# Decoder layer with experts: the last norm moved among the blocks of the last expert

## The chip, the core and the metric

The kernel runs on one core of a Trainium2 chip. The core has five engines with a queue of instructions each: TensorE (PE in the profile; PEld are its weight loads), VectorE (DVE), ScalarE (ACT), GpSimd (POOL) and SyncE (SP). In this kernel SP issues most plain transfers, and GpSimd issues the indirect ones, which gather or scatter rows by a table of row numbers. The metric is the time of one execution in microseconds; lower is better.

## The reference, cut to what matters

The reference is one decoder layer on 4 sequences of 512 tokens of 256 numbers: a state space mixer, an mLSTM attention over a context, and a feed-forward part with 8 experts, each followed by a residual addition and a layer norm. Only the last part matters here:

```python
logits = x @ gate_w
mult, sel = _sparse_mixer_routing(logits)       # two experts for each token
w = jnp.sum(mult[:, :, None] * (sel[:, :, None] == jnp.arange(E)[None, None, :]), axis=1)
h = jax.nn.silu(jnp.einsum('th,ehf->etf', x, w1)) * jnp.einsum('th,ehf->etf', x, w3)
out = jnp.einsum('etf,efh,te->th', h, w2, w)
...
x = _layernorm(x + _L0_ffn_ref(x, ...), axis=-1)
```

Each token goes through two of the eight experts; the two results, weighted, are added to the token's row, and the row is normed. There are 2048 rows, which the kernel handles as 16 tiles of 128.

## The kernel before, in words

After the first two layers, `close` writes the normed rows of each batch to `xd` (three copies in DRAM, of which the experts fetch) and to `yd`, the table in which the sums grow. `route` and `tables` put every token into lists: each expert has blocks of 128 tokens, with `tok` (which row to fetch), `wat` (which weight) and `dest` (which row to add to). Version 0 of the tables covers the first two batches, version 1 three, version 2 all four; version 3 holds overflow blocks, of which five (`NOV0`) are always run and up to 26 more behind a branch (L1668) that is not taken here.

A visit is an expert with one or more items; an item is one block of 128 rows or two. The order of visits is written by hand: `early` (experts 0 and 1, one block of version 0), `mid` (experts 2 to 7, blocks 0 and 1 of version 1), `late` (experts 6 down to 2, blocks 2 and 3, then the rest of experts 0 and 1, then the five overflow blocks). Each visit loads 3 MB of weights (`load_expert`, L1494, on SP, a ring of three). For each item, `fetch` gathers the rows (L1512, GpSimd), `turn` transposes them (L1578) and copies them out of PSUM (L1582), `up` multiplies by w1 and w3 (L1594), with Silu on ScalarE (L1599) and the product `ht` on VectorE (L1600), in four steps for a single block; three PSUM buffers (`pu`) stand between. `down` gathers the routing weights `wg` (L1611), multiplies by w2 (L1617), scales on ScalarE (L1621) and scatters with addition into `yd` (L1622). `work` runs `down` of an item after `up` of the next; the last `down` follows alone.

Only after all of this, and after the branch L1668, the sums are read back from `yd` into `x1` (L1676, four transfers of 512 KB), normed by `layer_norm` in four groups of four tiles (L63, L64, L66, L68, L73) and stored (L1681). A last branch (L1696) jumps over a slower exact form of the whole layer, which is not taken either.

The kernel is written with a framework that decides the order of the instructions on each engine by its own estimate of when each can start, and that adds the waits. What stands in the source in one place can therefore stand elsewhere on the engine's queue; where the text speaks of the built order, it means the order in the compiled program. [...] One case of this is the end of the second layer for batch 3: GpSimd adds the residual (L1076, four additions), VectorE takes its statistics (L63, `n2st`), while the first expert blocks already run on PE.

Of the kernel before, what the change touches and what calls it, by code (L numbers as in the profile page):

```python
# [9 lines left out]
F32 = mybir.dt.float32  # L10
AF = mybir.ActivationFunctionType
ALU = mybir.AluOpType
# [3 lines left out]
B, S, D = 4, 512, 256  # L16
# [26 lines left out]
def decoder_kernel(ctx: ExitStack, tc: tile.TileContext, t: dict, out: bass.AP):  # L43
    nc = tc.nc

    def pool(stack, name, bufs, psum=False):
        kw = {"space": PSUM} if psum else {}
        kw["reuse_waits"] = "tile"
        return stack.enter_context(tc.tile_pool(name=name, bufs=bufs, **kw))
# [28 lines left out]
    def layer_norm(sp, dst, src, n, tag):  # L78

        norm_apply(dst, src, n, *norm_stats(sp, src, n, tag))  # L80
# [1076 lines left out]
    def layers23(fast):  # L1157
# [4 lines left out]
        with ExitStack() as rest:  # L1162
# [360 lines left out]
            def static(v, e, *blocks):  # L1523
                return v, own(e, *blocks)

            early = [(e, [static(0, e, 0)]) for e in range(NEARLY)]
            mid = [(e, [static(1, e, 0, 1)]) for e in range(NEARLY, NE)]
            mid[-1][1].append(static(2, NE - 1, 2, 3))
            late = [(e, [static(2, e, 2, 3)]) for e in range(NE - 2, NEARLY - 1, -1)]
            late += [(e, [static(2, e, 1, 2), static(2, e, 3)]) for e in range(NEARLY)]  # L1530
            late += [((i,), [(3, [i])]) for i in range(NOV0)]
            rare = [((i,), [(3, [i])]) for i in range(NOV0, NOV)]

# [34 lines left out]
            xtp = pool(rest, "xt", 2)  # L1568
            np3 = pool(rest, "n3", 2)
            pup = pool(rest, "pu", 3, psum=True)  # L1570
# [13 lines left out]

            def up(xT_, G, w1, w3):

                N, U = G * P, TS // (G * P)
                ht = htp.tile([P, NF * G * P], F32, tag="ht", name="ht")
                for f in range(0, NF, U):
# [12 lines left out]
                    )  # L1602
                return ht.rearrange("p (f n) -> p f n", n=N)

            def down(v, cols, ht, w2):
                G = len(cols)
                ps = pop.tile([P, 2, D], F32, tag="po", name="po")
                y = yp.tile([P, 2, D], F32, tag="y", name="y")
                wg = xgp.tile([P, 2], F32, tag="wg", name="wg")
                for g, c in enumerate(cols):  # L1610
                    nc.gpsimd.indirect_dma_start(  # L1611
                        out=wg[:, g : g + 1], out_offset=None, in_=wds[min(v, 2)][:, :],
                        in_offset=bass.IndirectOffsetOnAxis(ap=wat[v][:, c : c + 1], axis=0),
                    )
                for g, c in enumerate(cols):
                    for f in range(NF):
                        nc.tensor.matmul(  # L1617
                            ps[:, g, :], ht[:, f, g * P : (g + 1) * P], w2[:, f, :],
                            start=(f == 0), stop=(f == NF - 1),
                        )  # L1620
                    nc.scalar.activation(y[:, g, :], ps[:, g, :], AF.Copy, scale=wg[:, g : g + 1])  # L1621
                    nc.gpsimd.indirect_dma_start(  # L1622
                        out=yd[:, :],
                        out_offset=bass.IndirectOffsetOnAxis(ap=dest[v][:, c : c + 1], axis=0),
                        in_=y[:, g, :], in_offset=None,
                        bounds_check=NT - 1, oob_is_err=False, compute_op=ALU.add,
                    )

            def work(visits, weights, ahead=(), between=None):


# [4 lines left out]
                for i, (n, v, cols) in enumerate(line):  # L1636
                    G = len(cols)
                    xT_ = turn(xgs.pop(0), G)
                    w1, w3, w2 = weights[n]
                    ht = up(xT_, G, w1, w3)  # L1640
                    if i + 2 < len(line):
# [6 lines left out]
                    if between is not None:  # L1648
                        between(i)
                down(*pending)  # L1650
                return weights[len(visits) :]

# [5 lines left out]
            else:  # L1658
                last = iter(())
            weights = work(early, weights, mid)  # L1660
            for _ in last:
                pass
            work(mid + late, weights, (), lambda i: overflow() if i == 1 else None)
            n_items = nc.values_load(
# [3 lines left out]
            with tc.If(n_items > NOV0):  # L1668
                work(rare, [weights_of(e) for e, _ in rare[:2]])


            NG = 4
            yv = yd.rearrange("(n p) d -> p n d", p=P)
            for g in range(NTT // NG):
                ns = slice(g * NG, (g + 1) * NG)
                nc.sync.dma_start(out=x1[:, ns, :], in_=yv[:, ns, :])  # L1676
            for g in range(NTT // NG):
                ns = slice(g * NG, (g + 1) * NG)
                ot = np3.tile([P, NG, D], F32, tag="ot", name="ot")
                layer_norm(np3, ot, x1[:, ns, :], NG, "n3")  # L1680
                nc.sync.dma_start(  # L1681
                    out=out_t[g * NG * P : (g + 1) * NG * P, :].rearrange("(i p) d -> p i d", p=P),
                    in_=ot,
                )

# [117 lines left out]
```

## Time and profile before

| What | us |
|---|---|
| Time, median of 3 runs (728.43 to 729.73) | 728.48 |
| The profiled execution's own time | 728.45 |
| Its span, first to last instruction | 726.5 |
| PE busy | 660.9 |
| VectorE busy | 303.9 |
| ScalarE busy | 230.7 |
| GpSimd busy | 220.7 |
| `up` matmuls (L1594), busy | 263.9 |
| `down` matmuls (L1617), busy | 135.3 |
| Scatters into `yd` (L1622), 37 of 1.61 | 59.7 |
| Mean granted clock of PE, as a share | 0.95 |

Busy times of engines overlap, so they do not add up to the span. What sets the end is read from two other views: the table of busy time in stretches of the execution, which tells where an engine has no gap, and the chain of work that ended last, which goes back from the last instruction to whatever released it. A line of the timeline shows start, duration, engine, line of the source, operation, what is written and read, and in brackets the idle time before it and what ended it. Lines with a q behind the engine are its sequencer: branches, semaphores, drains.

### The profile page before, as it was taken

The numbers are of one execution on the slowest core, as the hardware profiler recorded it, in microseconds if no ns is written. First come the engines' busy times: TensorE is split into PE (matmuls) and PEld (weight loads), VectorE is DVE, ScalarE is ACT, GpSimd is POOL, SyncE is SP. The second block draws the span as 40 slices with busy tenths as digits, with TensorE's granted clock in tenths as the row PEclk, the third lists the DMA queues.
The fourth block names the chain that finished last, engine by engine and source line by source line (L and its number), as shares of the span: only waits on it lengthen the run. The fifth ranks groups of instructions, "written<-read, shape, count | busy, mean of one in ns | idle before, by whom it ended". The sixth has DMA issues, their size and how long they took to land. (4 is left out here: it accounts for less than half of the span.)

```text
span 726.5 us, 8949 instructions
## 1 busy us (share of the span) xinstructions
PE 660.9 (91%) x3319; PEld 497.4 (68%) x3319; DVE 303.9 (42%) x776; ACT 230.7 (32%) x450; POOL 220.7 (30%) x244
## 2 busy tenths in 40 slices
PE   5979879998999898899999999999999999999930
PEld 2413357765534444888888888888888898999920
DVE  0796855668364787864222111112211211212116
ACT  1438760224357574552122111111212111212110
POOL 0512231000135466463232333322223232241210
PEclk9999988999989899899999999999999999999975
DMA  8200050100910325697445463454545634358234
GB/s 279 95 1 0 1 174 0 30 30 14 323 40 1 117 65 177 196 325 239 154 160 177 129 193 87 145 164 162 164 119 187 192 80 139 119 149 300 72 84 163
DMA packets 62895, 95.32 MB, mean 131 GB/s; under 512 B 8713, under 2 KB 49489, under 8 KB 62577
## 3 DMA queue, kind: packets, MB, share of 16 engines
q1 hardware_dynamic: 53456, 83.39, 33.7%
q0 software_dynamic: 8288, 9.08, 7.1%
q10 hardware_dynamic: 1088, 2.10, 0.9%
q8 instruction: 30, 0.49, 0.3%
q14 instruction: 33, 0.26, 0.1%
HBM read 81.40 MB, written 13.80 MB: 131 GB/s over the span
## 5 line engine op out<-in xcount | busy, mean ns | idle before, releaser
L1594 PE MATMUL pu<-xgT,w 128*128 128x256 f32 (+1 forms) x1472 | 263.9, 340 | 0.5 <-issue 0.4
L1594 PEld LDWEIGHTS pu<-xgT,w 128*128 128x128 f32 x1472 | 237.4, 192 | 24.8 <-issue 0.6
L1600 DVE TENSOR_TENSOR ht<-pu,si 128x256 f32<-128x256 f32 x148 | 62.7, 424 | 241.0 <-ACT si L1599 240.9
L1617 PE MATMUL po<-w,ht 128*128 128x256 f32 x592 | 135.3, 380 | 0.3 <-DVE ht L1600 0.3
L1622 POOL DMA_INDIRECT yd<-y,dest x37 | 59.7, 1613 | 206.5 <-ACT y L1621 183.6
L1599 ACT ACTIVATE si<-pu 128x256 f32<-128x256 f32 x148 | 56.7, 384 | 202.1 <-PE pu L1594 202.1
L1617 PEld LDWEIGHTS po<-w,ht 128*128 128x128 f32 x592 | 109.5, 190 | 15.5 <-DVE ht L1600 0.7
L202 PE MATMUL xz<-xT,win 128*128 128x512 f32 x128 | 60.1, 625 | 10.5 <-DMA win<-in_win 8.2
L202 PEld LDWEIGHTS xz<-xT,win 128*128 128x128 f32 x128 | 24.7, 198 | 44.3 <-issue 39.2
L1512 POOL DMA_INDIRECT xg<-xd,tok x37 | 36.8, 995 | 54.9 <-PE pt L1578 38.7
L1621 ACT ACTIVATE y<-po,wg 128x256 f32<-128x256 f32 x37 | 17.5, 474 | 106.3 <-PE po L1617 106.3
L981 POOL TENSOR_TENSOR ct<-ct,tri 128x128 f32<-128x128 f32 x64 | 32.7, 529 | 47.1 <-ACT ct L980 44.5
L1611 POOL DMA_INDIRECT wg<-wd,wat x37 | 37.3, 1009 | 11.1 <-issue 10.2
L418 PE MATMUL fpy<-mt,xs 128*128 128x512 f32 (+3 forms) x128 | 39.3, 460 | 0.9 <-DVE fsz L422 0.8
L221 DVE SCALAR_TENSOR_TENSOR acc<-xp,convw,acc 128x2048 f32<-128x2048 f32 x12 | 30.7, 2571 | 22.3 <-POOL acc L216 22.2
L980 ACT ACTIVATE ct<-pq,eT 128x512 f32<-128x512 f32 (+3 forms) x64 | 30.6, 523 | 22.8 <-PE pq L970 22.7
L970 PE MATMUL pq<-x1T,ctxT 64*128 64x512 f32 (+3 forms) x128 | 34.0, 505 | 3.3 <-ACT ct L980 3.2
L418 PEld LDWEIGHTS fpy<-mt,xs 128*128 128x128 f32 x128 | 23.2, 201 | 13.6 <-issue 7.3
L988 PE MATMUL ph<-ct,val 128*64 128x512 f32 (+3 forms) x128 | 32.4, 491 | 0.0
L1582 DVE COPY xgT<-pt 128x512 f32<-128x512 f32 (+1 forms) x23 | 13.5, 586 | 42.5 <-PE pt L1578 42.4
L439 PE MATMUL fpo<-fwout,fsz 128*128 128x256 f32 x128 | 29.7, 392 | 0.0
L970 PEld LDWEIGHTS pq<-x1T,ctxT 64*128 64x128 f32 x128 | 13.7, 193 | 22.8 <-ACT ct L980 10.9
(254 smaller groups left out, 596.9 us busy)
## 6 DMA issues: line engine op xcount, KB each, us to landing
w<-in_w SPq DMA_DIRECT2D x60, 1024.0 KB
xd<-x SPq DMA_DIRECT2D x9, 512.0 KB
xT<-in_xT ACTq DMA_DIRECT2D x4, 512.0 KB
ctxT<-in_ctxT SPq DMA_DIRECT2D x1, 2048.0 KB
val<-in_ctx SPq DMA_DIRECT2D x4, 512.0 KB
fxr<-in_x SPq DMA_DIRECT2D x4, 512.0 KB
yd<-x SPq DMA_DIRECT2D x4, 512.0 KB
x<-yd SPq DMA_DIRECT2D x4, 512.0 KB
```

Of the source, the lines that this page charges most:

```text
L202: nc.tensor.matmul(ps, win[:, k, c * P : (c + 1) * P], xT[:, k, b * S : (b + 1) * S], start=(k == 0), stop=(k == 1),)
L418: nc.tensor.matmul(ps[:, j * P :], xs[j][:, c, :], mt[b][j], start=(j == 0), stop=(j == NB - 1),)
L970: nc.tensor.matmul(ps[:, :w], ctxT[rows, p, s0 : s0 + P], x1T[rows, p, s0 : (b + 1) * S], start=True, stop=True,)
L981: nc.gpsimd.tensor_tensor(ct[:, :P], ct[:, :P], tri, ALU.mult)
L988: nc.tensor.matmul(po[DH * e : DH * (e + 1), tb * P :], val[:, b * NB + tb, 2 * p + e, :], cts[e], start=(tb == 0), stop=(tb == NB - 1),)
L1512: nc.gpsimd.indirect_dma_start(out=xg[:, g, :], out_offset=None, in_=xds[min(v, 2)][:, :], in_offset=bass.IndirectOffsetOnAxis(ap=tok[v][: ...
L1594: nc.tensor.matmul(ps[:, j, u, :], w[:, k, (f + u) * P : (f + u + 1) * P], xT_[:, k, :N], start=(k == 0), stop=(k == 1),)
L1599: nc.scalar.activation(si, ps[:, 0].rearrange("p u n -> p (u n)"), AF.Silu)
L1600: nc.vector.tensor_tensor(ht[:, f * N : (f + U) * N], ps[:, 1].rearrange("p u n -> p (u n)"), si, ALU.mult)
L1611: nc.gpsimd.indirect_dma_start(out=wg[:, g : g + 1], out_offset=None, in_=wds[min(v, 2)][:, :], in_offset=bass.IndirectOffsetOnAxis(ap=wat ...
L1617: nc.tensor.matmul(ps[:, g, :], ht[:, f, g * P : (g + 1) * P], w2[:, f, :], start=(f == 0), stop=(f == NF - 1),)
L1622: nc.gpsimd.indirect_dma_start(out=yd[:, :], out_offset=bass.IndirectOffsetOnAxis(ap=dest[v][:, c : c + 1], axis=0), in_=y[:, g, :], in_of ...
```

## The change

Expert 2 (`NEARLY`) leaves `mid` and `late` and becomes the visit `final`, with four items of one block each, behind the overflow blocks. `finale` runs it. The pending `down` of the last overflow block is issued inside the first of those blocks. Then the routing weights of all four blocks are gathered (`weigh`, into `wgf`), the sums of all 2048 rows are read back (`load_sums`), and the rows of the four blocks are gathered from `yd` into `ys`. From the second block on, each of the four steps of `up` is followed by a piece of `norm_all`: statistics of two tiles, then normed rows, half of them on VectorE (`apply`) and half on ScalarE (`apply2`), in place in `x1`, and the stores. So every row is normed and stored, also those to which expert 2 still has something to add. For these, `settle` adds the weighted product of the block to the gathered rows and takes their statistics, and `put` norms them and scatters them over the output. The branch for more overflow blocks comes last; if it were taken, the sums of expert 2 would be added to `yd`, and all rows would be normed and stored again.

In the listing of the diff, "..." marks what is left out; `normed` also holds the buffers, `down` now calls `weigh`, `product` and `scatter`, which do what its own lines did before.

```diff
-            mid = [(e, [static(1, e, 0, 1)]) for e in range(NEARLY, NE)]
+            mid = [(e, [static(1, e, 0, 1)]) for e in range(NEARLY + 1, NE)]
             mid[-1][1].append(static(2, NE - 1, 2, 3))
-            late = [(e, [static(2, e, 2, 3)]) for e in range(NE - 2, NEARLY - 1, -1)]
+            late = [(e, [static(2, e, 2, 3)]) for e in range(NE - 2, NEARLY, -1)]
             late += [(e, [static(2, e, 1, 2), static(2, e, 3)]) for e in range(NEARLY)]
             late += [((i,), [(3, [i])]) for i in range(NOV0)]
+
+            final = (NEARLY, [static(1, NEARLY, 0), static(1, NEARLY, 1)])
+            final[1].extend([static(2, NEARLY, 2), static(2, NEARLY, 3)])
             rare = [((i,), [(3, [i])]) for i in range(NOV0, NOV)]
...
-            np3 = pool(rest, "n3", 2)
+            np3 = pool(rest, "n3", 1)
+            fin = pool(rest, "fin", 1)
...
-            def up(xT_, G, w1, w3):
+            def up(xT_, G, w1, w3, ht):
 
                 N, U = G * P, TS // (G * P)
-                ht = htp.tile([P, NF * G * P], F32, tag="ht", name="ht")
...
-                return ht.rearrange("p (f n) -> p f n", n=N)
+                    yield
+
+            def inner(G):
+                return htp.tile([P, NF * G * P], F32, tag="ht", name="ht")
+
+            def weigh(wg, v, c):
+                nc.gpsimd.indirect_dma_start(
+                    out=wg, out_offset=None, in_=wds[min(v, 2)][:, :],
+                    in_offset=bass.IndirectOffsetOnAxis(ap=wat[v][:, c : c + 1], axis=0),
+                )
...
+            def product(ps, g, G, ht, w2):
+                for f in range(NF):
...
+            def scatter(rows, v, c, src, **kw):
+                return nc.gpsimd.indirect_dma_start(
+                    out=rows[:, :],
+                    out_offset=bass.IndirectOffsetOnAxis(ap=dest[v][:, c : c + 1], axis=0),
+                    in_=src, in_offset=None, bounds_check=NT - 1, oob_is_err=False, **kw,
+                )
...
-                down(*pending)
-                return weights[len(visits) :]
+                return weights[len(visits) :], pending
...
+                def stats(i, src):
+                    nc.vector.bn_stats(out=st[:, i, :], in_=src)
+                    nc.vector.bn_aggr(out=mv[:, i, :], in_=st[:, i, :])
+
+                def scales(i, j):
+                    nc.scalar.activation(sd[:, i:j], mv[:, i:j, 1], AF.Sqrt, bias=eps5)
+                    nc.vector.reciprocal(rs[:, i:j], sd[:, i:j])
+
+                def shifts(i, j):
+                    nc.vector.scalar_tensor_tensor(
+                        ms[:, i:j], mv[:, i:j, 0], -1.0, rs[:, i:j], ALU.mult, ALU.mult
+                    )
+
+                def apply(i, row, src=None):
+                    nc.vector.tensor_scalar(
+                        row, row if src is None else src, mv[:, i, 0:1], rs[:, i : i + 1], ALU.subtract, ALU.mult
+                    )
+
+                def apply2(i, row):
+                    nc.scalar.activation(
+                        row, row, AF.Identity, bias=ms[:, i : i + 1], scale=rs[:, i : i + 1]
+                    )
...
+            def load_sums():
+                for g in range(0, NTT, NG):
+                    nc.sync.dma_start(out=x1[:, g : g + NG, :], in_=yv[:, g : g + NG, :])
+
+            def store(g):
+                return nc.sync.dma_start(out=ov[:, g : g + NG, :], in_=x1[:, g : g + NG, :])
...
+            def finale(visit, weights, pending):
...
+                def norm_all():
+
+                    half = NTT // 2
+                    for h in range(2):
+                        for i in range(h * half, (h + 1) * half):
+                            stats(i, x1[:, i, :])
+                            if h and i % 2:
+                                apply(i - half - 1, x1[:, i - half - 1, :])
+                                apply2(i - half, x1[:, i - half, :])
+                                if i % NG == NG - 1:
+                                    store(i - half - NG + 1)
+                            if i % 2:
+                                yield
+                        if h == 0:
+                            scales(0, half)
+                            shifts(0, half)
+                    yield
+                    scales(half, NTT + 2)
+                    shifts(half, NTT + 2)
+                    for i in range(half, NTT, 2):
+                        apply(i, x1[:, i, :])
+                        apply2(i + 1, x1[:, i + 1, :])
+                        if i % NG == NG - 2:
+                            store(i + 2 - NG)
+                            yield
+                    for i in range(2):
+                        put(i)
+
+                def put(i):
+                    apply(NTT + i, ro[:, i, :], ys[:, i, :])
+                    v, (c,) = line[i]
+                    sent.append(scatter(out_t, v, c, ro[:, i, :]))
...
+                def settle(i, ps):
+                    nc.vector.scalar_tensor_tensor(
+                        ys[:, i, :], ps, wg[:, i : i + 1], ys[:, i, :], ALU.mult, ALU.add
+                    )
+                    stats(NTT + i, ys[:, i, :])
+
+                norm = norm_all()
+                xgs = [fetch(*it) for it in line[:2]]
+                hts = []
+                for i, (v, (c,)) in enumerate(line):
+                    xT_ = turn(xgs.pop(0), 1)
+                    hts.append(inner(1))
+                    for q, _ in enumerate(up(xT_, 1, w1, w3, hts[-1])):
+                        if q == 0:
+                            if i == 0:
+                                down(*pending)
+                                for j, (v_, (c_,)) in enumerate(line):
+                                    weigh(wg[:, j : j + 1], v_, c_)
+                                load_sums()
+                                for j, (v_, (c_,)) in enumerate(line):
+                                    nc.gpsimd.indirect_dma_start(
+                                        out=ys[:, j, :], out_offset=None, in_=yd[:, :],
+                                        in_offset=bass.IndirectOffsetOnAxis(
+                                            ap=tok[v_][:, c_ : c_ + 1], axis=0
+                                        ),
+                                    )
+                            else:
+                                ps = pop.tile([P, 2, D], F32, tag="po", name="po")
+                                product(ps[:, 0, :], 0, 1, hts[i - 1], w2)
+                                settle(i - 1, ps[:, 0, :])
+                            if i + 2 < N:
+                                xgs.append(fetch(*line[i + 2]))
+                        if i:
+                            next(norm, None)
+                for _ in norm:
+                    pass
+                scales(rows[N - 2], rows[N - 2] + 1)
+                put(N - 2)
+                ps = pop.tile([P, 2, D], F32, tag="po", name="po")
+                product(ps[:, 0, :], 0, 1, hts[-1], w2)
+                settle(N - 1, ps[:, 0, :])
+                scales(rows[N - 1], rows[N - 1] + 1)
+                put(N - 1)
+                return ys, sent
...
-            work(mid + late, weights, (), lambda i: overflow() if i == 1 else None)
+            weights, pending = work(
+                mid + late, weights, [final], lambda i: overflow() if i == 1 else None
+            )
+            ys, sent = finale(final, weights[0], pending)
             n_items = nc.values_load(
                 items, min_val=0, max_val=NOV,
                 skip_runtime_bounds_check_because="it is a sum of at most NOV items",
             )
             with tc.If(n_items > NOV0):
-                work(rare, [weights_of(e) for e, _ in rare[:2]])
-            NG = 4
-            yv = yd.rearrange("(n p) d -> p n d", p=P)
-            for g in range(NTT // NG):
-                ns = slice(g * NG, (g + 1) * NG)
-                nc.sync.dma_start(out=x1[:, ns, :], in_=yv[:, ns, :])
-            for g in range(NTT // NG):
-                ns = slice(g * NG, (g + 1) * NG)
-                ot = np3.tile([P, NG, D], F32, tag="ot", name="ot")
-                layer_norm(np3, ot, x1[:, ns, :], NG, "n3")
-                nc.sync.dma_start(
-                    out=out_t[g * NG * P : (g + 1) * NG * P, :].rearrange("(i p) d -> p i d", p=P),
-                    in_=ot,
-                )
+                for i, (v, (c,)) in enumerate(final[1]):
+                    scatter(yd, v, c, ys[:, i, :])
+                _, pending = work(rare, [weights_of(e) for e, _ in rare[:2]])
+                down(*pending)
+                stats, scales, shifts, apply, apply2 = normed(0)
...
```

## The prediction

> **What bounds the kernel now.** I read the table of busy time by stage first, then the chain that ended last, then the timeline of GpSimd, VectorE and PE around 310 to 320 us, then GpSimd's sequencer at the end. The stage table's columns are stretch, length, busy us of PE, PE's weight loads, VectorE, ScalarE, GpSimd, then PE's granted clock, DMA share and GB/s:
>
> ```profile
> 300.00:321.00 21.00, 20.73 (x160) 19.43 (x159) 13.56 (x66) 10.79 (x20) 12.20 (x13) 1.00 0.80 288
> 321.00:697.00 376.00, 374.76 (x1992) 334.24 (x1990) 81.17 (x211) 74.07 (x181) 117.93 (x98) 1.00 0.51 155
> 697.00:726.50 29.50, 0.00 (x0) 0.00 (x0) 12.39 (x52) 2.47 (x5) 1.56 (x1) 0.52 0.48 151
> ```
>
> The expert stage (321 to 697) is PE at full clock with hardly a gap: every us that PE is made to wait there is paid, and what other engines do beside it is free. Then come 29.5 us without PE. The chain (start, us, what) says what fills them:
>
> ```profile
> 682.67 20.21 DMA yd<-y,dest
> 702.88 0.02 issue
> 702.89 4.02 DMA x<-yd
> ...
> 719.41 0.41 DVE ot L73
> ```
>
> PE's last product ends at 696.15 (its group starts at 689.94 and lasts 6.21); the last scatter starts at 697.43 and lands 3.7 later; the sums are read back from 702.89; VectorE norms from 706.93 to 719.82; then 6.7 us for the last store and the program's end. That tail is 726.5 - 696.15 = 30.35 us.
>
> GpSimd's own end is off the path today, but it decides what follows:
>
> ```profile
> L1668 POOLq INC_SWDGE_SEM  x1: 1574/1574/1574, 701.4 to 701.4; - x1
> L1696 POOLq COMPARE_BRANCH  x1: 45/45/45, 703.4 to 703.4; - x1
> L1696 POOLq EVENT_SEMAPHORE  x6: 17/30/43, 707.7 to 708.2; - x6
> L1799 POOLq DRAIN  x1: 5750/5750/5750, 709.8 to 709.8; - x1
> ```
>
> (ns min/median/max, first and last start.) After its last scatter lands (701.2) its queue passes the unused branch L1668 (1.57 us of semaphore work), jumps over the exact path (L1696, 703.4 to 707.7), does 1.57 us more and drains until 715.55: 14.3 us from landing to drained. The final barrier takes 0.8 us after the last arrival (725.7 to 726.5).
>
> **The change, part by part.** Blocks of expert 2 are 0 to 3; t counts from block 0's first up-projection matmul.
>
> *Expert 2 goes last, in four single blocks.* A double visit takes PE 21.16 us (381.10 to 402.26, from one up-projection to the next, is the row), a single block 10.82 (671.98 to 682.80): 4 x 10.82 - 2 x 21.16 = +0.95 us. One load of 3 MB falls away; PE waits for no weights now, so that is worth nothing. Where t = 0 lies: the last overflow item's up-projection moves from 682.80 to 640.48; 7.14 us of it, 2.6 of the product before, 0.22 of transposes and 0.87 of its own product put t = 0 at 651.3, other delays not counted.
>
> *Weights of expert 2's rows gathered early.* In the built order the two gathers of wgf for blocks 0 and 1 stand on GpSimd's queue directly ahead of the residual additions of batch 3 (L1076), behind two like them of today:
>
> ```profile
> 311.95 0.94 POOL L1611 DMA_INDIRECT wg<-wd,wat  x1 [0.30 <-issue]
> 312.92 2.79 POOL L1076 TENSOR_TENSOR hv<-hv,x 128x256 f32<-128x256 f32 x4
> 313.69 0.43 DVE L63 BATCH_NORM_STATS2 n2st<-hv 128x6 f32<-128x256 f32 x1 [2.95 <-POOL hv L1076]
> 318.93 0.42 DVE L1600 TENSOR_TENSOR ht<-pu,si 128x256 f32<-128x256 f32 x1
> 319.41 1.13 PE L1617 MATMUL po<-w,ht 128*128 128x256 f32 x4 [0.28 <-DVE ht L1600]
> ```
>
> hv starts the moment GpSimd is free; VectorE waits for it, and behind that wait stands the product ht for which PE already waits. Two gathers at 0.94 + 0.31 us are +2.5 us on PE's path; 0 if something else were late too, 2.8 at most. No gap after 322 gives it back. The wgf gathers of blocks 2 and 3 wait for the last routing tables (written by 333.4), where GpSimd then idles until 356: nothing.
>
> *The norm of all rows inside the last blocks.* The last overflow product ends at t = 4.38; its scatter starts at 5.2 and lands at 8.95. The read-back is issued then, at 9.1, no longer behind the L1668 branch; its first quarter is there 4.02 later (t = 13.2), the others 1.5 us apart (0.5 MB at the 345 to 376 GB/s of 705 to 710). GpSimd's four row gathers wait for the same landing; behind them stand only the output scatters, since the blocks' rows are fetched ahead; gathers of this size land 4.3 after issue, so the first is there at 13.5. In the built order VectorE takes six statistics ahead of ht of block 1's first quarter, and all of the following ahead of the copy of block 2's transposed rows: sixteen statistics at 0.39, three ht at 0.40, the first settle 0.45 with its statistic 0.39, four applies at 0.33, two small ones 0.33, the copy 0.42: 10.35 us, so the copy ends at 23.6 to 24.2. PE wants it at 2 x (1.79 + 2.59 + 5.36) + 2 x (0.22 + 0.86) = 21.64. PE stands 2.2 us; 1.5 if the quarters come early, 4 if the row gathers push in front of them. The other waits are covered: three PSUM buffers let ht of block 1 come at 18.8 (it comes at 15.9); ScalarE's seven more table loads (1.28 us each, the row at 306.39) and eight Identity rows of 0.53 end before the ht that needs them; the stores are issued by t = 36 and land by 41, and three of the four output scatters (1.9 us each) follow by 47.
>
> *The tail.* PE ends at 4 x 9.74 + 3 x 1.08 + 3.45 + 2.2 = 47.85. Settle 0.45, statistics 0.39 + 0.17, root 0.30, reciprocal 0.18, apply 0.41, semaphores and issue 0.55: the last scatter starts 2.5 later. It lands in 3.7 (the row of the last yd scatter; 3.2 to 5.2 over the quiet ones), and now GpSimd's end is on the path, 14.3 + 0.8. The tail is 2.5 + 3.7 + 15.1 = 21.3 us against 30.35: -9.05.
>
> Here the Trainium skill is weighed ("VectorE: DVE Perf Modes", The DRAIN you can't avoid): it gives the drains of the program's end as some 12 ns, constant, on all five engines. Four engines agree (7 to 17 ns), GpSimd's row is 5750. By the rule the tail would be 15.6 us; I take the row, since the same instructions stand ahead of it in both kernels.
>
> Sum: -9.05 + 0.95 + 2.5 + 2.2 = -3.4. Span 726.5 - 3.4 = 723.1; the profiled execution took 728.45 for its 726.5, with the median of the runs at 728.48, so 723.1 + 1.95 = 725.1 us.
>
> **PE's clock.** Both stalls cut dense matmuls for 2 to 3 us. The skill ("TensorE: Matmul & The Clock Gate", Why this matters for your kernels) allows gaps up to about 3 us before a window of idling halves the clock; by it they cost only themselves. The trace shows less patience:
>
> ```profile
> 241.00:242.00 1.00, 0.03 (x1) 0.06 (x1) 1.00 (x2) 1.00 (x4) 0.95 (x1) 0.53 0.00 0
> 247.00:248.00 1.00, 1.00 (x4) 0.78 (x5) 1.00 (x5) 0.34 (x2) 0.00 (x0) 0.56 1.05 344
> ```
>
> The granted clock (third from the end) fell to half with a gap of 1.2 us behind it and one of 1.9 just begun, and came back 6.8 us later; around 288, with PE as idle, it stayed whole. A fall costs PE half of 3.4 to 6.8 us, 1.7 to 3.4. By the rule the sum stays at -3.4, by the row it is up to +3.4; I keep the rule for the likeliest number and put the row into the range.
>
> **Rivals.** (1) *Slower than before, through the clock*: both stalls halve it for 6.8 us each: 725.1 + 2 x 3.4 = 731.9. It decides once it costs 4.9 us, one long fall and one short. For it the fall at 241; against, no single gap in dense work has an example here. (2) *A longer stall ahead of block 2*: the read-back's quarters wait behind the row gathers; 3 us more gives 728.1, no change. For it: beside weight loads a scatter took 7.8 us to land; against: no weights are loading then. (3) *GpSimd's drain belongs to something that no longer runs*: 725.1 - 5.7 = 719.4. (4) *The early gathers are hidden*, a part that does nothing: 722.6.
>
> **How the numbers follow.** My forecast, with rival 4 and up to one short fall of the clock, 722 to 727: 0.54. Rival 3: 0.12, all faster. Rival 2, between 727 and 730: 0.13. Rival 1 and still longer stalls, above 730: 0.21. A measurement of this kernel can't tell 0.2% (1.5 us) from nothing, so faster is below 727.0 and slower above 730.0: 0.66, 0.13, 0.21. The range, 719.4 to 731.0, leaves out half of rival 1 and part of rival 3.
>
> **What would show it.** Right: VectorE's first n2st of batch 3 at about 316.2 after 5.4 us of waiting for hv; PE idle near 319 to 322; one gap of some 2 us ahead of block 2, ended by the copy of transposed rows; the last output scatter near 704; a chain that ends in GpSimd's queue with a drain of 5 to 6 us. Wrong: PE gap-free in the last expert, a clock below 1.00 after a gap, stores landing after the last scatter could start, or a drain of some ns.

## The result and the profile after

The changed kernel takes 719.15 us (median of 4 runs, 718.58 to 719.62); the kernel before took 728.45 beside it (727.90 to 729.73). The ratio is 0.987, with a 95% interval of 0.9852 to 0.9887. Forecast were 725.1 us and a range of 719.4 to 731.0: the direction was right, the gain of 9.3 us is nearly three times the 3.4 us that I had summed, and the time lies just below the range. The profiled execution took 718.58 for a span of 716.7 (forecast 723.1).

The table of busy time by stage of the changed kernel, with the columns as for the kernel before (length; busy us of PE, its weight loads, VectorE, ScalarE, GpSimd; PE's granted clock, DMA share, GB/s):

```profile
300.00:321.00 21.00, 18.49 (x137) 17.05 (x136) 12.93 (x63) 9.38 (x17) 13.13 (x14) 1.00 0.80 282
321.00:701.20 380.20, 378.65 (x2131) 340.75 (x2131) 95.33 (x271) 87.25 (x198) 118.26 (x100) 1.00 0.51 157
701.20:716.70 15.50, 0.00 (x0) 0.00 (x0) 1.67 (x5) 0.29 (x1) 0.98 (x1) 0.60 0.08 17
```

PE stays the bound to 701.2, some 5 us longer than before, and the stretch without PE shrank from 29.5 us to 15.5, of which VectorE works 1.67. The chain that ended last (start, us, what) now ends in GpSimd's work:

```profile
658.94 3.69 DMA yd<-y,dest
...
663.61 6.66 DMA x<-yd
...
676.47 0.34 DVE xgT L1586
676.82 0.14 issue
676.95 2.02 PE pu L1597 x16
...
697.74 3.47 PE po L1619 x16
701.21 0.02 issue
701.24 0.50 DVE ys L1763
...
703.42 0.50 POOLq L1822
703.92 0.71 POOL out L1625
```

The scatter of the last overflow block lands at 662.63, a load of the sums lands at 670.27, VectorE's statistics and rows follow, and the copy of block 2's transposed rows ends at 676.81; PE has waited 1.54 us for it. The timeline shows this wait, and the earlier one of VectorE for the residual rows (`hv`), behind the early gathers:

```profile
315.10 0.43 DVE L63 BATCH_NORM_STATS2 n2st<-hv 128x6 f32<-128x256 f32 x1 [5.46 <-POOL hv L1076]
...
676.95 2.02 PE L1597 MATMUL pu<-xgT,w 128*128 128x128 f32 x16 [1.54 <-DVE xgT L1586]
```

Behind PE's last product come settle, statistics, root, apply and the last scatter. Its issue starts at 703.65 on the timeline; the chain puts the start 0.27 later. What follows on GpSimd's sequencer (ns min/median/max, first and last start; the drain line also holds two short ones) is not in the chain, but takes the rest of the span:

```profile
L1826 POOLq EVENT_SEMAPHORE  x4: 17/43/4112, 704.5 to 708.8; - x4
L1826 POOLq INC_SWDGE_SEM  x1: 598/598/598, 708.9 to 708.9; - x1
L1859 POOLq COMPARE_BRANCH  x1: 45/45/45, 709.9 to 709.9; - x1
L1859 POOLq EVENT_SEMAPHORE  x6: 17/30/43, 713.0 to 713.4; - x6
L1859 POOLq INC_SWDGE_SEM  x1: 576/576/576, 713.5 to 713.5; - x1
L1962 POOLq DRAIN  x3: 46/107/1748, 714.1 to 716.4; - x3
```

The same instructions as before, with other lengths: the two semaphore steps take 0.60 and 0.58 us instead of 1.57 each, the drain 1.75 instead of 5.75. From the landing (708.8) to the end of the drain (715.85) it is 7.1 us, where I had put 14.3.

### The profile page after: what moved, and what is told of

Its sections match the earlier page's. It is cut to its first block, busy times and chain, and to the rows that moved or that the text cites. A ratio compares the mean times of both kernels' runs of the same rounds, so it can differ in the third digit from the quotient of the medians.

```text
span 716.7 us, 9223 instructions
## 1 busy us (share of the span) xinstructions
PE 663.3 (93%) x3447; PEld 502.6 (70%) x3447; DVE 307.1 (43%) x788; ACT 240.2 (34%) x460; POOL 220.4 (31%) x248
## 5 line engine op out<-in xcount | busy, mean ns | idle before, releaser
L1597 PE MATMUL pu<-xgT,w 128*128 128x128 f32 (+1 forms) x1600 | 266.6, 327 | 1.6 <-DVE xgT L1586 1.5
L1597 PEld LDWEIGHTS pu<-xgT,w 128*128 128x128 f32 x1600 | 243.2, 193 | 23.9 <-ACT si L1602 1.9
L1625 POOL DMA_INDIRECT yd<-y,dest x33 | 53.3, 1616 | 146.6 <-ACT y L1639 127.0
L1639 ACT ACTIVATE y<-po,wg 128x256 f32<-128x256 f32 x33 | 15.6, 474 | 92.5 <-PE po L1619 92.5
L1612 POOL DMA_INDIRECT wg<-wd,wat x33 | 32.6, 989 | 9.9 <-issue 9.6
L1586 DVE COPY xgT<-pt 128x256 f32<-128x256 f32 (+1 forms) x25 | 13.8, 551 | 41.6 <-PE pt L1582 41.6
```

The costliest lines, as they stand in the source:

```text
L1597: nc.tensor.matmul(ps[:, j, u, :], w[:, k, (f + u) * P : (f + u + 1) * P], xT_[:, k, :N], start=(k == 0), stop=(k == 1),)
L1612: nc.gpsimd.indirect_dma_start(out=wg, out_offset=None, in_=wds[min(v, 2)][:, :], in_offset=bass.IndirectOffsetOnAxis(ap=wat[v][:, c : c + ...
L1625: return nc.gpsimd.indirect_dma_start(out=rows[:, :], out_offset=bass.IndirectOffsetOnAxis(ap=dest[v][:, c : c + 1], axis=0), in_=src, in_ ...
```

## The experiments

The experiments ran on different chips, on which the kernel before took from 727.8 to 735.3 us. Times are therefore compared only with runs beside them on the same chip, and most readings are lengths inside a trace. The listings of the edits are shortened.

### What sets the length of GpSimd's end: four suspects taken one at a time

The kind of the last transfer, in the changed kernel and, turned round, in the kernel before:

```diff
-                    sent.append(scatter(out_t, v, c, ro[:, i, :]))
+                    kw = dict(compute_op=ALU.add) if i == N - 1 else {}
+                    sent.append(scatter(out_t, v, c, ro[:, i, :], **kw))
```

> The changed kernel, with one difference: the last of the four output scatters adds to the rows it meets, as the scatters into yd do (so the rows of that block come out as a sum of two normed rows). Theory A (the kind of GpSimd's last transfer sets how long its end takes): the issue takes 1.6 us, the two semaphore steps 1.57 each, the drain 5.75; from landing to drained 14.3 us instead of 7.1, span 716.7 + 0.6 + 7.2 = 724.5. Theory B (VectorE's work beside it slows GpSimd's end) and theory C (the transfers of the sums and of the output beside it do): steps of 0.6, drain of 1.75, span 717.3.

```diff
+                    kw = dict(compute_op=ALU.add) if adds else {}
...
-                        bounds_check=NT - 1, oob_is_err=False, compute_op=ALU.add,
+                        bounds_check=NT - 1, oob_is_err=False, **kw,
...
-                down(*pending)
+                down(*pending, adds=between is None)
```

> The kernel before, with one difference: the last scatter of the last overflow block writes its rows instead of adding them (so those rows lack their other parts). Theory A: the two semaphore steps fall to 0.6 us each and the drain to 1.75, though the norm still follows; GpSimd is done at about 708 instead of 715.6, and the time is at most 1 to 1.5 us shorter (an issue of 1.0 instead of 1.6, and the read-back stands behind the first semaphore step), since VectorE sets the end. Theories B and C: steps of 1.57, drain of 5.75, GpSimd done at 715.

VectorE's work and the transfers beside it:

```diff
-                ot = np3.tile([P, NG, D], F32, tag="ot", name="ot")
-                layer_norm(np3, ot, x1[:, ns, :], NG, "n3")
...
-                    in_=ot,
+                    in_=x1[:, ns, :],
```

> The kernel before without the last norm: the sums are read back and stored as they are, so VectorE has nothing to do after 697 us. Theory B: GpSimd's drain falls to about 1.75 us. Theory A: it stays at 5.75, the semaphore steps at 1.57, and GpSimd's 715.6 + 0.8 sets the end near 716.4 to 718. Theory C: the drain stays long where the stores run beside it, and ends with them, near 715.

```diff
                 put(N - 1)
+                idle = fin.tile([P, 40, 6], F32, tag="idle", name="idle")
+                for i in range(40):
+                    nc.vector.bn_stats(out=idle[:, i, :], in_=ys[:, N - 1, :])
```

> The changed kernel, with 40 statistics of one and the same tile on VectorE behind the last output row (their results are not used): VectorE is busy from 703.4 to about 719 us, all through GpSimd's end. Theory B: semaphore steps of 1.57 and a drain above 5 us, GpSimd's end at 723, span 724. Theories A and C: steps of 0.6, drain of 1.75; VectorE's own end sets the span near 720 to 722.

Measured, in that order (kernel before beside them: 730.08): 719.35, 728.11, 722.61 and 722.62 us. The sequencer's drain in each, `last_adds`:

```profile
L1963 POOLq DRAIN  x3: 46/107/1748, 714.9 to 717.2; - x3
```

`last_plain`:

```profile
L1800 POOLq DRAIN  x3: 46/107/5750, 709.4 to 725.9; - x3
```

`no_last_norm`:

```profile
L1797 POOLq DRAIN  x3: 46/107/5750, 710.6 to 720.3; - x3
```

`vector_busy`:

```profile
L1965 POOLq DRAIN  x3: 46/107/1748, 717.5 to 720.5; - x3
```

To the nanosecond, each has the drain of the kernel that it was made from, and the first semaphore step too; the second differs by 2 to 4 ns (the two steps take 598 and 580, 1574 and 1565, 1574 and 1565, 598 and 580). A last transfer that adds or one that writes, VectorE busy or idle, many transfers beside it or fewer: none moves it. Theories A and B fall with this. In `vector_busy` VectorE ran to 719.25 while the drain began at 717.5. Against theory C stands that in `no_last_norm` the DMA share was 1.09 from 710 to 715, during the drain, against 0.46 in the kernel before, and the drain kept its length; `before_4_more`, below, settles it. What was left is something that the two programs differ in as a whole. The profile's list of transfers gives one: the kernel before issues 111 indirect transfers (37 each of `xg`, `wg`, `yd`), the changed one 115 (37, 33 and 33, and 4 each of `wgf`, `ys`, `out`).

### The number of indirect transfers

Further gathers of 128 weights, not used, each with one of the visits 6 to 11 of the list (counted from 0), where GpSimd idles:

```diff
                     if between is not None:
                         between(i)
+                        for k in range(n):      # n = 1, 4; in the changed kernel 13
+                            if i == 6 + k % 6:
+                                spare = xgp.tile([P, 2], F32, tag="spare", name="spare")
+                                nc.gpsimd.indirect_dma_start(
+                                    out=spare[:, 0:1], out_offset=None, in_=wds[2][:, :],
+                                    in_offset=bass.IndirectOffsetOnAxis(ap=wat[2][:, 0:1], axis=0),
+                                )
```

> The kernel before with one more indirect gather of 128 weights (not used), in the middle of the expert stage where GpSimd idles: 112 indirect transfers instead of 111. The first runs had semaphore steps of 1.57 us and a drain of 5.75 in every form of the kernel before, and of 0.6 and 1.75 in every form of the changed kernel, which issues 115. Theory D (the number of indirect transfers issued so far sets it): other values than 1.57 and 5.75, on a line through 111 and 115: 1.33 and 4.75. Theory E (it belongs to the code around the branches, not to the number): 1.57 and 5.75. The time is 728.5 to 730 in both.

> The kernel before with four more such gathers: 115 indirect transfers, as many as the changed kernel has. Theory D: semaphore steps of 0.6 us and a drain of 1.75, GpSimd done near 708.5. Theory E: 1.57 and 5.75, GpSimd done near 715.6. The time stays at 728.5 to 730, since VectorE sets the end here.

> The changed kernel with 13 more such gathers: 128 indirect transfers. Theory D: semaphore steps and drain change; where to depends on where the count starts again, with the end of the span moved by as much (a drain of 5.75 and steps of 1.57 would give 716.7 + 6 = 722.7). Theory E: 0.6 and 1.75, span 716.7 to 717.5.

They took 727.06, 726.45 and 719.81 us (kernel before beside them 728.23). `before_1_more` missed the straight line of theory D (steps of 1594 and 1585, drain 5832: up, not down), but it moved; `before_4_more` has the changed kernel's short end in the old program, with the last norm, the read-back and the stores all beside it as before:

```profile
L1675 POOLq INC_SWDGE_SEM  x1: 584/584/584, 700.2 to 700.2; - x1
L1806 POOLq DRAIN  x3: 46/107/1707, 706.4 to 724.4; - x3
```

and `after_13_more` is longer again, 818 and 2647. So the length goes up with further transfers, and down once between 112 and 115. Theories C and E are out. Two more runs, n = 2 and 3 in the kernel before, place the fall:

> The kernel before with two more gathers of 128 weights: 113 indirect transfers. The semaphore steps took 1574, 1594 and 584 ns at 111, 112 and 115 transfers, the drain 5750, 5832 and 1707. Theory D as a sawtooth that falls once between 112 and 115: either 1614 and 5914 (one more step of 20 and 82 up the line), or, if the fall is already past, 540 and 1540. An estimate puts the fall between: the Trainium skill (DMA Engines, The descriptor swizzle) counts 9 descriptors on each of the 16 engines for a transfer over 128 partitions, so that 113 transfers make 1017 and 114 make 1026; if the queue holds a round 1024, 113 is still long.

> The kernel before with three more such gathers: 114 indirect transfers. By the same estimate (1026 descriptors, past 1024): the fall is past, semaphore steps near 564 ns, drain near 1625. If the fall lies between 114 and 115: 1634 and 5996.

`before_2_more` (113 transfers):

```profile
L1675 POOLq INC_SWDGE_SEM  x1: 1614/1614/1614, 704.3 to 704.3; - x1
L1806 POOLq DRAIN  x3: 46/107/5913, 712.8 to 728.8; - x3
```

`before_3_more` (114 transfers):

```profile
L1675 POOLq INC_SWDGE_SEM  x1: 574/574/574, 707.4 to 707.4; - x1
L1806 POOLq DRAIN  x3: 46/107/1667, 714.4 to 731.4; - x3
```

| Indirect transfers | First step, ns | Drain, ns | Kernel |
|---|---|---|---|
| 111 | 1574 | 5750 | before, and two variants of it |
| 111 | 1588 | 5791 | `plain_weights` (below) |
| 112 | 1594 | 5832 | before, 1 more |
| 113 | 1614 | 5913 | before, 2 more |
| 114 | 574 | 1667 | before, 3 more |
| 115 | 584 | 1707 | before, 4 more |
| 115 | 598 | 1748 | changed, and its variants with 115 |
| 128 | 818 | 2647 | changed, 13 more |

One step over the edge takes 1.04 us from each semaphore step and 4.25 from the drain, 6.3 together. At an equal number the changed program is still 14 ns longer in the first step and 41 in the drain than the kernel before (both at 111 and at 115), so the number is nearly, but not quite, all that counts. The added transfers, and those taken away, were all gathers of 128 weights; transfers of another shape were not tried.

The edge lies where the estimate in the expectation had it. The Trainium skill ("DMA: Bandwidth & Descriptors", The descriptor swizzle) counts 9 read and 9 write descriptors per engine for one transfer of 1 MiB to 128 partitions. Taken over, as an estimate, for each of these smaller transfers, that makes 1017 for 113 of them and 1026 for 114. That they fill a ring of 1024 entries fits, but it stays a guess: only one edge was seen, and no trace here counts descriptors. These two runs took 731.17 and 733.94 us (kernel before 731.15); in the kernel before, GpSimd's end is covered, so their times say nothing of it.

### Back to 111 in the changed kernel, and the two other terms

The four gathers of `wgf` as plain loads of SyncE; the same four from the last tables; each block transposed during the block before; and the last two together:

```diff
-                                    weigh(wg[:, j : j + 1], v_, c_)
+                                    nc.sync.dma_start(out=wg[:, j : j + 1], in_=wds[min(v_, 2)][0:P, :])
```

> The changed kernel, with the four gathers of wgf replaced by plain loads on SyncE's queue (the first 128 entries of the weight table instead of the listed ones, so expert 2's part is weighted wrongly). 111 indirect transfers, as in the kernel before. Theory D (GpSimd's end grows with the number of indirect transfers and falls somewhere between 112 and 115): semaphore steps of 1.57 us and a drain of 5.75 are back, 5.9 us more at the end than the changed kernel has. The two gathers ahead of the residual additions are gone too: PE comes out of that place 1.4 us earlier by the trace of the changed kernel, 2.5 by my prediction. Sum 719.2 + 5.9 - 1.4 = 723.7, or 722.6. Theory E (the drain belongs to the code around the branches): 719.2 - 1.4 = 717.8, or 716.7.

```diff
-                                    weigh(wg[:, j : j + 1], v_, c_)
+                                    weigh(wg[:, j : j + 1], 2, c_)
```

> The changed kernel, with all four gathers of wgf made from the last routing tables, so that none can stand ahead of the residual additions of batch 3; still 115 indirect transfers. My prediction's term: 719.2 - 2.5 = 716.7. By the changed kernel's trace (PE stands 2.13 + 0.38 us there, 0.28 before, and its next up-projection is 1.85 later relative to the kernel before, of which the front's own drift is open): 719.2 - 1.4 to - 2.2 = 717.0 to 717.8. The rival that these gathers are hidden: 719.2.

```diff
+                ahead = turn(xgs.pop(0), 1)
                 for i, (v, (c,)) in enumerate(line):
-                    xT_ = turn(xgs.pop(0), 1)
+                    xT_, ahead = ahead, None
                     hts.append(inner(1))
                     for q, _ in enumerate(up(xT_, 1, w1, w3, hts[-1])):
+                        if q == 0 and i + 1 < N:
+                            ahead = turn(xgs.pop(0), 1)
```

> The changed kernel, with each block's rows transposed and copied while the block before begins, so that the copy of block 2's rows no longer stands behind sixteen statistics on VectorE. My prediction's term (2.2) as the trace of the changed kernel has it: PE's gap of 1.54 us ahead of block 2 goes, 719.2 - 1.5 = 717.7. Rival: the wait returns at another place, since the product ht stands behind the same statistics and ScalarE's Silu behind their root: 719.2.

> The changed kernel with both edits: wgf gathered from the last tables, and each block's rows transposed while the block before begins. The two places do not touch each other, so the gains add: 719.2 - 1.4 - 1.5 = 716.3, or 715.2 with my prediction's 2.5 for the gathers. If one of them is given back at the end: 717.7.

Medians: 724.56 (718.09 to 727.59), 719.76 (718.45 to 720.65), 723.07 (719.25 to 725.12) and 719.31 (716.03 to 722.22), with the kernel before at 733.01 (731.40 to 735.13). Spreads this wide, and no run of the changed kernel beside them, decide little by time. `plain_weights` decides by its trace: with 111 transfers the changed program has the long end back.

```profile
L1826 POOLq INC_SWDGE_SEM  x1: 1588/1588/1588, 710.1 to 710.1; - x1
L1859 POOLq INC_SWDGE_SEM  x1: 1566/1566/1566, 715.2 to 715.2; - x1
L1962 POOLq DRAIN  x3: 46/107/5791, 716.8 to 723.1; - x3
```

From the start of its last scatter (705.49) to the end of the span (723.4) it takes 17.9 us; `late_weights`, with 115, takes 12.2 (705.80 to 718.0). The two steps make 2.0 of the difference of 5.7 and the drain 4.0; the jump over the exact path is 0.4 shorter.

For the other two terms the runs were repeated on one chip, with the changed kernel beside them:

> The changed kernel itself, so that the next three can be held against it on one chip: 719.2, if this chip is like the first.

> The changed kernel with all four gathers of wgf made from the last routing tables. Counted within one trace, the way from the product group ahead of the place (309.35 before, 308.26 after) to the first up-projection of the next visits (321.98, 323.83) took 12.63 us before and 15.57 after, and two groups further 19.21 and 22.61; PE's granted clock fell to 0.74 and 0.83 there. If the two gathers are the cause of both, the way takes 12.6 and 19.2 again, the clock stays at 1.00, and the time is 3.4 us below the changed kernel's. My prediction's term: 2.5 below it. If they are hidden: the same.

> The changed kernel with each block's rows transposed while the block before begins. On the earlier chip PE's gap ahead of the up-projection of block 2 did not go: it was 1.17 to 1.21 us and ended by the product ht instead of the copy. So the rival (the wait returns at another place): 0.3 us below the changed kernel; my prediction's term as measured: 1.5 below it.

> Both edits together: 3.4 + 0.3 = 3.7 us below the changed kernel if the gathers cost 3.4 and the stall only moves, 4.9 if the stall goes. A ratio of 0.982 to 0.981 to the kernel before.

Changed kernel 722.14 (720.61 to 723.21), late weights 721.27 (719.99 to 722.32), turned early 722.60 (720.58 to 725.35), both 721.30 (719.77 to 723.46), kernel before 733.30. None of the three can be told from the changed kernel here. The traces say why for the gathers: on this chip PE had gaps of up to 1.15 us in its issue of matmuls between 308 and 316 us, in both forms, and VectorE came to the residual rows without having to wait for them. The stall did not go; it got another cause, much as the rival had it. In `turned_early_2` PE still stands ahead of block 2's up-projection, for 1.08 us instead of 1.54. The rows are there in time, and it waits for `ht` instead. Steps 2 to 4 of block 1 and step 1 of block 2 on PE, then the first and the second `ht` of block 1 on VectorE:

```profile
675.24 5.52 PE L1597 MATMUL pu<-xgT,w 128*128 128x128 f32 x48
681.85 2.05 PE L1597 MATMUL pu<-xgT,w 128*128 128x128 f32 x16 [1.08 <-DVE ht L1603]
```

```profile
674.45 0.40 DVE L1603 TENSOR_TENSOR ht<-pu,si 128x256 f32<-128x256 f32 x1
...
681.39 0.40 DVE L1603 TENSOR_TENSOR ht<-pu,si 128x256 f32<-128x256 f32 x1
```

With three PSUM buffers (`pu`), the first step of block 2 needs the buffer that the second `ht` of block 1 sets free, and that `ht` stands behind the statistics on VectorE, 6.9 us after the first.

The last run was one more trace of the late weights, on a chip without those gaps:

> The changed kernel with all four gathers of wgf made from the last routing tables, once more, for its trace alone. On the chips of the last timed calls PE was late around 310 us for a reason of its own (gaps in its issue), with and without these gathers. In the traces without those gaps, from the product group ahead of the place to the first and the third group of up-projections of the next visits: 12.6 and 19.2 us in five forms of the kernel before, 15.5 to 15.6 and 22.5 to 22.6 in four forms of the changed kernel. If this chip shows none of the gaps and the two gathers are the cause: 12.6 and 19.2 again, clock 1.00 throughout. If something else of the change is: 15.5 and 22.6. If the gaps are there, the question stays open.

It took 716.78 us (kernel before 727.76). PE's timeline in the changed kernel first:

```profile
308.26 0.60 PE L1619 MATMUL po<-w,ht 128*128 128x256 f32 x2
...
320.82 1.13 PE L1619 MATMUL po<-w,ht 128*128 128x256 f32 x4 [2.13 <-DVE ht L1603]
323.83 3.57 PE L1597 MATMUL pu<-xgT,w 128*128 128x256 f32 x12
...
330.87 14.41 PE L1597 MATMUL pu<-xgT,w 128*128 128x256 f32 x66
```

The same groups in `late_weights_3`:

```profile
310.81 0.60 PE L1619 MATMUL po<-w,ht 128*128 128x256 f32 x2
...
320.87 1.13 PE L1619 MATMUL po<-w,ht 128*128 128x256 f32 x4 [0.28 <-DVE ht L1603]
323.43 2.83 PE L1597 MATMUL pu<-xgT,w 128*128 128x256 f32 x12 [0.39 <-issue]
...
330.02 5.34 PE L1597 MATMUL pu<-xgT,w 128*128 128x256 f32 x24
```

And in the kernel before:

```profile
309.35 0.60 PE L1617 MATMUL po<-w,ht 128*128 128x256 f32 x2
...
328.56 16.79 PE L1594 MATMUL pu<-xgT,w 128*128 128x256 f32 x77
```

From the first row to the last it is 22.61 us with the gathers ahead of `hv`, 19.21 without them, and 19.21 in the kernel before. `last_adds` and `vector_busy`, two forms of the changed kernel on the same chip as `late_weights_3`, take 22.56 and 22.62, so the chip is not the cause. The two gathers cost 3.4 us where PE has no gap of its own. Part of it is the clock. The stage table of the changed kernel:

```profile
316.00:320.00 4.00, 2.31 (x10) 1.38 (x8) 3.86 (x27) 3.33 (x6) 1.12 (x2) 1.00 1.02 385
320.00:324.00 4.00, 3.18 (x18) 2.64 (x19) 2.02 (x8) 3.97 (x8) 2.26 (x2) 0.74 0.69 219
324.00:328.00 4.00, 4.00 (x19) 3.49 (x20) 4.00 (x14) 1.93 (x4) 2.96 (x4) 0.83 0.65 159
```

and of `late_weights_3`:

```profile
320.00:324.00 4.00, 3.32 (x23) 2.47 (x22) 2.51 (x10) 3.97 (x8) 2.21 (x2) 1.00 1.05 376
324.00:328.00 4.00, 4.00 (x26) 3.56 (x25) 3.97 (x16) 2.28 (x4) 3.14 (x3) 1.00 0.75 205
```

Behind gaps of 0.38 and 2.13 us the granted clock fell: (1 - 0.74) x 4 x 2 + (1 - 0.83) x 4 x 2 = 3.4 us at half speed. Without the long gap it stays at 1.00. The rows tell the two parts of the cost apart. Up to the product group at the end of the wait (320.82, 320.87, and 319.41 in the kernel before) it is 12.56 us with the gathers and 10.06 without: 2.5, two gathers at 1.25. Behind it, where the clock is low, it is 10.05 and 9.15: the other 0.9.

## Why the prediction was wrong

The step that failed is in the tail: "now GpSimd's end is on the path, 14.3 + 0.8". That it would be on the path was right; its length was taken over unchanged "since the same instructions stand ahead of it in both kernels". The same instructions do stand there, but their length follows how many indirect transfers the program has issued, and the change takes that number from 111 to 115, across the edge between 113 and 114. It measured 7.1 us in place of 14.3. Of the 7.2, two semaphore steps make 2.0 and the drain 4.0 (shown by the table above, and by `plain_weights` in the changed program itself). The last 1.2 us is the jump over the exact path, 3.1 us from branch to first semaphore instead of 4.3. It takes 4.2 to 4.8 us in all forms of the kernel before, where the sums are read back at that time, and 2.5 to 3.1 in all forms of the changed one, where nothing is; that the transfers cause it was not tried.

So 6.0 us of the gain are luck: they come from the number of transfers, which the change altered in passing, and not from moving the norm. Without them the span would be near 722.7 (716.7 + 6.0, an estimate). That this is close to the 723.1 forecast is in part luck too, since the other errors below nearly cancel.

I had every number needed for a warning: a drain of 5750 ns against the Trainium skill's some 12 ns ("VectorE: DVE Perf Modes", The DRAIN you can't avoid). It was right to refuse the rule (1667 to 5913 ns on GpSimd in these runs), but a row without a known cause is not a constant. Rival 3 came nearest in time (719.4); its mechanism, a drain that belongs to something no longer run, is not what happened. Four more transfers, not fewer, made the drain short.

Step by step against the span (predicted 723.1, measured 716.7):

- *Four single blocks, +0.95.* Block 0's up-projection starts at 653.61 and block 1's at 664.42, 10.81 apart: as predicted.
- *Early gathers, +2.5.* Measured 3.4. VectorE waited 5.46 us for `hv` (predicted 5.4); the extra 0.9 is the clock. I had kept the rule of gaps up to 3 us (the Trainium skill, "TensorE: Matmul & The Clock Gate", Why this matters for your kernels) for the likeliest number and put the trace's row at 241 us into the range; the row was right. Block 0's start was still where I put it (653.8), because the profiled execution happened to reach this place 1.1 us earlier than the one before (308.26 against 309.35).
- *Stall ahead of block 2, +2.2.* Measured 1.54, ended by the copy as described; the clock stayed at 1.00 behind it. The first quarter of the sums was there at t = 13.0 (predicted 13.2).
- *Tail up to the last scatter, 2.5.* Measured 2.45 (701.2 to 703.65). The scatter was seen landed 5.1 us after its start instead of 3.7; the forms of the changed kernel range from 3.9 to 5.1. The barrier took the 0.8.

The sum of the corrections is -1.1 + 0.9 - 0.7 + 1.4 - 7.2 = -6.7 against the measured -6.4; 0.3 us in the blocks is not accounted for.

Rival 1, the slower one, had half of its mechanism confirmed: one of the two stalls halved the clock, for 0.9 us instead of 3.4, and the other did not. Rival 2 did not come. Rival 4 (hidden gathers) is wrong in all traces in which PE has no gaps in its issue around 310 us, as in the one that the forecast was made from; where it has them, the runs could not tell it from the others.

The late weights are the best version in the trace: the change without its 3.4 us. In time that is not shown: 716.78 us in one run is 0.985 of the kernel before beside it, where the changed kernel has 0.987, and in five runs of each on another chip, 721.27 against 722.14, the gain is not separated from the spread.

## What to carry to other kernels

When a change brings an engine's closing work onto the path, ask what that work's length depends on, and give it a range of its own unless two programs show the same length. A transfer that a scheduler moves to where an engine idles by its estimate can stand ahead of the one instruction that the bound engine waits for; gathering it from a table that is ready later was a one-word cure here. A copy moved out of a crowded stretch of an engine's queue frees little (here 1.54 us of waiting became 1.08) if the next thing that the bound engine needs stands in the same stretch.

## What the hardware showed that I had not expected

- GpSimd's closing drain and its semaphore steps behind a branch grew with each indirect transfer issued (drain 5750, 5832, 5913 ns at 111, 112, 113) and fell by 4.25 and 1.04 us at the 114th. Beyond the edge the slope was smaller at first (1667 to 1707 from 114 to 115) and 69 ns per transfer from 115 to 128.
- PE's clock halved for 3.4 us behind a gap of 2.13 us that had one of 0.38 ahead of it, inside otherwise dense work (320 to 328 us), and did not behind a single gap of 1.54 us (676.95). The length of one gap does not tell: in `late_weights` the longest gaps ahead of a granted clock of 0.50 (312 to 316 us) were 0.34 to 0.44 us (308 to 310), and gaps of up to 0.44 us in `plain_weights` (310 to 316) left it at 1.00. In the kernel before, the falls last 3.4, 6.8 or 10.2 us (223 to 228, 241 to 248, 104 to 115, summed over rows of 1 us). What decides was not tried.
- An indirect scatter that adds takes 1.6 us to issue and one that writes 1.0 for the same rows: 1.59 us in `last_adds` against 0.98 in the changed kernel, and 1.56 in the kernel before against 1.04 in `last_plain`.
